# Alternating long and short query blocks, with GpSimd adding the two attention maps and TensorE transposing one tensor of the long blocks

## The chip, the cores and the metric

The kernel runs on one core of a Trainium2 chip. The metric is device time in microseconds (us) for one execution of the program; the kernel before took 1212.99 us, the median of three runs (1210.94 to 1213.68). The engines are called TensorE (PE in the profile, its weight loads PEld), VectorE (DVE), ScalarE (ACT), GpSimd (POOL) and SyncE (SP). All data are 32-bit floats, apart from masks and a few constants. The profiles show TensorE's granted clock as a share of full speed.

## The reference, cut to what matters

Eight sequences of 512 tokens with 128 features each go through one layer. First a causal attention with 16 heads of 8 features, which takes the difference of two softmaxes over the same queries:

```python
s1 = einsum('bhqd,bhkd->bhqk', q, k1) * SCALE      # causal mask on both
s2 = einsum('bhqd,bhkd->bhqk', q, k2) * SCALE
attn = softmax(s1) - sigmoid(lambda_logit) * softmax(s2)
attn = attn / max(sum(|attn|), 1e-6)
out = (attn @ v) @ Wo.T
x = layernorm(x + out)
```

Then a mixture of experts: eight experts of 128 -> 512 -> 128 with a SiLU, of which each token uses the two that its router scores highest, a residual and a second layer norm. Of the two softmaxes the kernel keeps the unnormalised exponentials e1 and e2 and works with e1 - c2*e2, where c2 is a ratio per row; dividing by the sum of absolute values makes the common factor drop out.

## The kernel before, in words

**Units, slots, rounds.** A sequence b is cut into 16 units j of 32 queries; because the attention is causal, unit j needs the first L = 32(j+1) keys. The 16 heads stand as four groups g of four heads, and four heads by 32 queries fill the 128 partitions. A unit with L up to 256 is *early* (short): it has two slots, each with two groups and both score sets. A unit with L over 256 is late (long): it has four slots, each with two groups and one score set. So a sequence has 8*2 + 8*4 = 48 slots, and each is worked in one *round* (`round_of`). Four units make a block of 128 queries; there are 32 blocks.

**What a round does.** The schedule is written by hand: the order of calls in `round_of` is the order on every engine's queue. One round (1) multiplies a finished unit by v (`times_v`, L490), (2) lets TensorE compute the scores of the next slot (`scores`, L327 and L336, into one of two PSUM buffers `sc`), (3) lets ScalarE copy the last piece's transposed attention out of PSUM (`evacuate`, L473, from the single buffer `pt`), (4) takes the negated row maxima of this slot on VectorE (`maxima`, L349 and L357), (5) transposes the piece that was combined in the round before (`transposes`, L448), (6) runs the VectorE steps that were put aside, (7) combines pieces (`combine`), (8) takes the exponentials on ScalarE with their row sums (`exps`, L367), and (9) issues one step of each side job: block tasks, routing, indirect DMAs on GpSimd, expert matmuls.

**A piece** is two groups of an early unit or one group of a late one. `combine` lets VectorE read e1 and e2 once to get the row sums of max(c2*e2, e1) (`junk`, L393), and then GpSimd scales e2 in place by -c2 (L403). The sum e1 - c2*e2 is not formed there: for every 128 keys `transposes` turns both tensors, the second accumulating on the first in PSUM, so that the sum comes out of TensorE already transposed. Keys that do not fill 128 are gathered by a GpSimd copy (`rest`, L417).

**After four units** (in the order of j, so every 16 or 8 rounds a block ends) the block's results stand in one PSUM bank `po`; ScalarE copies them (`oraw`, L508) and the block tasks (`block_tasks`: normalise, project with Wo, layer norm, router logits) follow, one per round, from the queue `misc`.

**Experts.** Blocks are collected in order into chunks of 6, 9, 9, 6 and 2 blocks. When a chunk is complete, `route_tasks` finds the two experts of each token, and for the first four chunks GpSimd sends every token's row to two places in a DRAM tensor `xs` with indirect DMAs (`send`, L777; two for each block, one per round, all sends of a chunk write the same tensor), so that the rows of one expert stand together. Three empty steps later `go` puts the chunk's expert tiles in the queue `experts`: 19 tiles of 128 rows for 6 blocks and 25 for 9. Each tile loads its weights and rows on SP's queue, is transposed (L871), multiplied (`pz`, L900), passed through the SiLU (L845, L847) and multiplied again (`pa`, L880). A pace, worked out from the expected arrival of the next chunk, says how many expert steps a round gets. Afterwards GpSimd fetches each token's two rows (`fetch`, L925). The last chunk of 2 blocks is dense: all its tokens go through all experts (`pzd`, `py`).

**Side jobs tied to a unit.** The next sequence's x is loaded when unit 6 opens, and its five projection tasks go into `misc` when unit 8 opens.

**Buffers.** The exponentials `et` (three of full width), `aT` (two), the sums of a block (three).

Of the kernel before, what the change touches and what calls it, by code (L numbers as in the profile page):

```python
# [20 lines left out]
def kernel(  # L21
# [22 lines left out]
    Q = 32  # L44
# [67 lines left out]
    with ExitStack() as actx:  # L112
# [3 lines left out]
        ep = actx.enter_context(tc.tile_pool(name="ep", bufs=3))  # L116
        tp = actx.enter_context(tc.tile_pool(name="tp", bufs=2))
        op = actx.enter_context(tc.tile_pool(name="op", bufs=1))
# [17 lines left out]
        stage = ep.tile([P, 2, NP, 128], F32, tag="et", name="stage")  # L136
# [69 lines left out]
        class Chunk:  # L206


            def __init__(self, n0, nb, sparse):
                self.n0, self.nb, self.sparse = n0, nb, sparse  # L210
                self.xh = self.lg = None
                if sparse:
                    self.nt = tiles_of(nb)
                    self.xs = dram.tile([self.nt * P, D], F32, name=f"xs_{n0}")
                    self.ys = dram.tile([self.nt * P, D], F32, name=f"ys_{n0}")
# [11 lines left out]
        zero = aw.tile([P, D], F32, name="zero")  # L227
        chunks, n0 = [], 0
        for nb in (6, 9, 9, 6):
            chunks.append(Chunk(n0, nb, True))  # L230
            n0 += nb
        for n0 in range(n0, NB, 2):
            chunks.append(Chunk(n0, 2, False))
        chunk_of = {n: c for c in chunks for n in range(c.n0, c.n0 + c.nb)}
# [59 lines left out]
        class Unit:  # L294


            def __init__(self, b, j, blk):
# [11 lines left out]
                self.et = ep.tile([P, NG, 2, T], F32, tag="et", name=f"et_{b}_{j}")  # L309
                self.aT = self.c2 = self.rest = None  # L310

# [73 lines left out]
            def combine(self, piece):  # L385
# [16 lines left out]
                for g in piece:  # L402
# [7 lines left out]
                    )  # L410
                for gs, lo, kw in self.blocks(piece):
                    if len(gs) > 1:
                        if self.rest is None:
# [4 lines left out]
                            self.rest[:, :, gs[0] * kw : (gs[-1] + 1) * kw].rearrange(  # L418
                                "p s (g l) -> p s g l", l=kw
                            ),  # L420
                            self.et[:, gs[0] : gs[-1] + 1, :, lo : lo + kw].rearrange(
# [17 lines left out]
            def transposes(self, piece):  # L439

                pt = ps_t.tile([P, 4, P], F32, tag="pt", name=f"pt_{self.b}_{self.j}_{piece[0]}")
                for x_, (gs, lo, kw) in enumerate(self.blocks(piece)):
                    for k in range(2):
                        if len(gs) == 1:
                            lhsT = self.et[:, gs[0], k, lo : lo + kw]
                        else:
# [6 lines left out]
                            start=(k == 0),  # L453
# [4 lines left out]
            def evacuate(self, piece, pt):  # L458
                if self.aT is None:
                    self.aT = tp.tile([P, NG * NT, P], F32, tag="aT", name=f"aT_{self.b}_{self.j}")  # L460
# [19 lines left out]
            def times_v(self):  # L480
# [3 lines left out]
                if "po" not in self.blk:  # L484
                    self.blk["po"] = ps_o.tile([P, JT, P], F32, tag="po", name=f"po_{self.b}_{self.i}")
                for kb in range(self.n):
                    kw = min(P, self.L - P * kb)
                    v, rows = (vr[kw], P) if kw in vr else (vt, kw)
                    for g in range(NG):
                        nc.tensor.matmul(  # L490
                            self.blk["po"][32 * g : 32 * g + 32, self.jj, :],
# [4 lines left out]
                        )  # L496

        def block_tasks(b, i, blk):
# [5 lines left out]
            lg, ci = ch.lg, n - ch.n0  # L504

            def reciprocals():
                s["oraw"] = op.tile([P, JT, P], F32, tag="oraw", name=f"oraw_{n}")
                nc.scalar.copy(s["oraw"], blk["po"])  # L508
# [14 lines left out]
            def normalise():  # L523
                pm = ps_m.tile([P, JT, P], F32, tag="pm", name=f"pmr_{n}")
                for jj in range(JT):
# [7 lines left out]
                        s["oraw"].rearrange("p j (h q) -> p j h q", q=Q),  # L533
# [280 lines left out]
        def last_tasks(ch, c, acc):  # L814

            n = ch.n0 + c
# [138 lines left out]
        def dense_tasks(ch):  # L955
# [6 lines left out]
            def hidden(e, half):  # L962
# [25 lines left out]
                silu_doubled(pz, h, name, *((tp, "aT") if e in whole else (hp, "th")))  # L988
# [57 lines left out]
        to_combine, to_transpose, to_evacuate, to_multiply = deque(), deque(), deque(), deque()  # L1046

        def after_blocks(u):
            u.times_v()
            if u.jj == JT - 1:  # L1050
                tasks = block_tasks(u.b, u.i, u.blk)

                tasks[0]()
                misc.extend(tasks[1:])
                n = u.b * NT + u.i
                ch = chunk_of[n]
                if n == ch.n0 + ch.nb - 1:
# [5 lines left out]

        def times():

            at, now, ends = [], 0.0, {}
            for n in range(NB):
                for j in range(n % NT * JT, (n % NT + 1) * JT):
                    L = (j + 1) * Q
                    now += 2 * time_of(4 * L) if L <= T // 2 else 4 * time_of(2 * L)  # L1070
                ends[n] = now
            seq = now / B
            for ch in chunks:

                behind = seq * (24 + (2 * ch.nb + 3 if ch.sparse else 0)) / 48
# [205 lines left out]
```

## Time and profile before

| what | us |
|---|---|
| median of three runs | 1212.99 |
| the profiled execution, device time | 1212.04 |
| its span | 1210.1 |
| TensorE busy | 1093.9 |
| VectorE busy | 927.1 |
| ScalarE busy | 780.4 |
| GpSimd busy | 526.8 |
| start of the span to the first exponentials | 19 |
| the eight sequences' attention, with side jobs | 1070 |
| after the last exponentials | 121 |

The profile lists the busy time of each engine, and it can be asked for the same in any stretch of the span; the last three rows come from the start of the first and the end of the last exponentials (L367). Matmuls are pipelined, and a busy TensorE is not TensorE at its peak: eight transposes of 296 ns each stand in 1.09 us. A group of instructions is listed by its line, with its number, its busy time, the mean of one, and the idle time of its engine ahead of it. The profiled execution was 1.94 us longer than its span and 0.95 us shorter than the median.

### The profile page before, as it was taken

The page shows a single profiled execution, that of the slowest core. Times are in us where ns is not written, and L with a number is a line of the kernel's source. Part 1 is how long each engine was busy: PE and PEld are TensorE (multiplying, and loading weights), DVE is VectorE, ACT ScalarE, POOL GpSimd, SP SyncE. Part 2 cuts the span into 40 slices and gives each one's busy share as a digit, 9 for nine tenths or more (in the row PEclk, how much of TensorE's full clock was granted, in tenths as well). Part 3 has the DMA queues.
Part 4 walks back from the last instruction along what each step waited for, and adds up shares of the span by engine and source line. Part 5 has one row for each costly group of instructions (what it writes and reads, how often), then busy time and mean ns, then how long its engine had stood idle before and what let it go on. Part 6 is the DMA issues. An engine that isn't in the chain of part 4 may idle for free.

```text
span 1210.1 us, 28192 instructions
## 1 busy us (share of the span) xinstructions
PE 1093.9 (90%) x9450; PEld 776.2 (64%) x9450; DVE 927.1 (77%) x2837; ACT 780.4 (64%) x2775; POOL 526.8 (44%) x935
## 2 busy tenths in 40 slices
PE   5999899989999899989998999988999989997686
PEld 3566565555666566666666666666667667777675
DVE  4688778777887887987887878887767898874556
ACT  3678767576777777766766867774567566662221
POOL 4343433463423442267464432333554652444333
PEclk7699969797999999989998999997899799998998
DMA  4400000110221112100322222221213344444762
GB/s 133 122 8 1 10 2 8 31 56 30 50 63 46 54 32 67 45 27 27 93 69 58 73 54 68 64 73 31 81 52 91 95 120 124 122 123 129 207 177 67
DMA packets 128895, 84.28 MB, mean 70 GB/s; under 512 B 22896, under 2 KB 114288, under 8 KB 128752
## 3 DMA queue, kind: packets, MB, share of 16 engines
q1 hardware_dynamic: 111952, 68.26, 20.2%
q0 software_dynamic: 3840, 7.87, 2.3%
q10 hardware_dynamic: 12960, 6.36, 1.8%
q8 instruction: 75, 1.23, 0.4%
q14 instruction: 68, 0.56, 0.2%
HBM read 63.31 MB, written 17.56 MB: 67 GB/s over the span
## 4 chain that ended last, share of the span: by engine, by line
PE 60%; DVE 16%; ACT 11%; issue 6%; POOL 4%; DMA 3%; ACTq 1%; POOLq 0%; SPq 0%; DVEq 0%
PE pt L448 19%; PE sc L327 13%; ACT et L367 7%; PE po L490 5%; PE pz L900 5%; PE pa L880 5%; PE sc_None L327 5%; DVE junk L393 2%; DVE nm L357 2%; PE pmo L541 2%; ACT aT L473 2%; DVE nm L349 2%; POOL et L403 1%; DVE hT L847 1%; POOL xs L777 1%
## 5 line engine op out<-in xcount | busy, mean ns | idle before, releaser
L403 POOL TENSOR_SCALAR et<-et,c 128x224 f32<-128x224 f32 (+15 forms) x512 | 270.9, 534 | 458.1 <-DVE junk L393 295.0
L448 PE MATMUL pt<-ident,et 128*128 128x128 f32 (+1 forms) x2048 | 326.7, 296 | 26.8 <-ACT aT L473 14.9
L448 PEld LDWEIGHTS pt<-ident,et 128*128 128x128 f32 (+1 forms) x2048 | 230.5, 145 | 159.6 <-issue 58.2
L367 ACT ACTIVATE et<-sc,nm 128x512 f32<-128x512 f32 (+7 forms) x512 | 300.4, 595 | 48.7 <-DVE nm L357 27.6
L357 DVE TENSOR_REDUCE nm<-sc 128x2 f32<-128x576 f32 (+7 forms) x256 | 252.0, 984 | 45.1 <-PE sc L336 44.6
L473 ACT COPY aT<-pt 128x384 f32<-128x384 f32 (+5 forms) x488 | 186.1, 407 | 134.5 <-PE pt L448 130.7
L393 DVE SCALAR_TENSOR_TENSOR junk<-et,c 128x224 f32<-128x224 f32 (+15 forms) x512 | 258.6, 505 | 9.6
L327 PE MATMUL sc<-kT,qb 32*128 32x384 f32 (+7 forms) x1024 | 246.8, 559 | 10.9 <-ACT et L367 9.6
L367 ACT ACTIVATE et<-sc_None,nm 128x256 f32<-128x256 f32 (+7 forms) x512 | 188.6, 387 | 32.0 <-DVE nm L349 22.0
L327 PE MATMUL sc_None<-kT,qb 32*128 32x512 f32 (+7 forms) x512 | 116.5, 535 | 21.8 <-ACT et L367 21.0
L900 PE MATMUL pz<-xgT,w 128*128 128x128 f32 x704 | 102.1, 291 | 18.8 <-DVE xgT L874 18.5
L349 DVE TENSOR_REDUCE nm<-sc_None 128x4 f32<-128x256 f32 (+7 forms) x128 | 96.1, 751 | 29.6 <-PE sc_None L336 29.3
L327 PEld LDWEIGHTS sc<-kT,qb 32*128 32x128 f32 x1024 | 78.3, 187 | 61.3 <-ACT et L367 27.4
L367 ACT ACTIVATION_READ_ACCUMULATOR et<-sc_None,nm 128x1 f32 x512 | 108.1, 211 | 0.0
L900 PEld LDWEIGHTS pz<-xgT,w 128*128 128x128 f32 x704 | 92.5, 204 | 23.6 <-DVE xgT L874 21.2
L367 ACT ACTIVATION_READ_ACCUMULATOR et<-sc,nm 128x1 f32 x512 | 103.9, 203 | 0.0
L880 PE MATMUL pa<-w,hT 128*128 128x128 f32 x704 | 98.1, 285 | 0.6 <-ACT ysb L890 0.6
L845 ACT ACTIVATE th<-pz 128x512 f32<-128x512 f32 x88 | 52.7, 599 | 68.9 <-PE pz L900 47.9
L880 PEld LDWEIGHTS pa<-w,hT 128*128 128x128 f32 x704 | 90.9, 202 | 1.3 <-ACT ysb L890 0.7
L777 POOL DMA_INDIRECT xs<-xh,row x60 | 65.9, 1099 | 46.9 <-DMA xs<-xh,row 31.3
L490 PE MATMUL po<-aT,vt 128*32 128x128 f32 (+1 forms) x2048 | 85.3, 290 | 0.0
L847 DVE SCALAR_TENSOR_TENSOR hT<-th,pz 128x512 f32<-128x512 f32 x88 | 60.2, 684 | 30.8 <-ACT th L845 30.6
(150 smaller groups left out, 1281.0 us busy)
## 6 DMA issues: line engine op xcount, KB each, us to landing
w<-in_w_dram SPq DMA_DIRECT2D x192, 256.0 KB
xg<-xs SPq DMA_DIRECT2D x88, 64.0 KB
ys<-ysb ACTq DMA_DIRECT2D x88, 64.0 KB
xs<-zero SPq DMA_DIRECT2D x2, 1600.0 KB
xs<-zero SPq DMA_DIRECT2D x2, 1216.0 KB
xt<-in_x_dram SPq DMA_DIRECT2D x8, 256.0 KB
out_dram<-ot SPq DMA_DIRECT2D x32, 64.0 KB
vr<-vt SPq DMA_DIRECT2D x32, 32.0 KB
```

The lines of the kernel that those rows point to most:

```text
L327: nc.tensor.matmul(parts[gi][:, :, :L], lhsT=qb[r, j].rearrange("p h q -> p (h q)"), rhs=kT[r, sets, :L], start=True, stop=False,)
L349: nc.vector.tensor_reduce(self.nm[:, g, :], sc.rearrange("p g (s l) -> p g s l", s=2)[:, :, :, : self.L], AX.X, ALU.max, negate=True,)
L357: nc.vector.tensor_reduce(self.nm[:, g, s], sc[:, :, : self.L], AX.X, ALU.max, negate=True)
L367: nc.scalar.activation(self.et[:, g, si, : self.L], sc[:, gi, lo : lo + self.L], AF.Exp, bias=self.nm[:, g, si : si + 1], accum_out=self.b ...
L393: nc.vector.scalar_tensor_tensor(junk[:, :L], self.et[:, g, 1, :L], self.c2[:, g : g + 1], self.et[:, g, 0, :L], ALU.mult, ALU.max, accum_ ...
L403: nc.gpsimd.tensor_scalar(self.et[:, g, 1, :L], self.et[:, g, 1, :L], self.c2[:, g : g + 1], -1.0, ALU.mult, ALU.mult,)
L448: nc.tensor.matmul(pt[: len(gs) * kw, x_, :], lhsT=lhsT, rhs=ident, is_transpose=True, start=(k == 0), stop=(k == 1),)
L473: nc.scalar.copy(self.aT[: rows[done], self.used + done : self.used + end, :], pt[: rows[done], done:end, :],)
L490: nc.tensor.matmul(self.blk["po"][32 * g : 32 * g + 32, self.jj, :], lhsT=v[:rows, kb, 32 * g : 32 * g + 32], rhs=self.aT[:rows, self.at[g ...
L777: nc.gpsimd.indirect_dma_start(ch.xs[:, :], bass.IndirectOffsetOnAxis(ap=ch.row[:, k, c : c + 1], axis=0), ch.xh[:, c, :], None,)
L880: nc.tensor.matmul(pm[:, 1, :], lhsT=hT[y][:, f, :], rhs=w[y][1][:, f, :], start=(f == 0), stop=(f == NF - 1),)
L900: nc.tensor.matmul(pz[:, f, :], lhsT=w[t][0][:, f * P : (f + 1) * P], rhs=xgT[t], start=True, stop=True,)
```

## The change

It changes the order of the rounds, the work of a late piece, and what follows from both.

- **Order.** `rounds_of` yields two rounds of a late unit and one of an early one in turn: units 15 and 0 together, then 14 and 1, down to 8 and 7. The two lengths of a pair add up to 544 keys. A sequence still has 48 rounds.
- **A late piece.** After scaling e2 by -c2, GpSimd adds e1 to it in place (`tensor_add`, 256 instructions on 288 to 512 columns). `transposes` and the `rest` copy then take the one tensor. Early pieces are as before. One piece is combined in each round.
- **Results of a unit.** `po` holds one unit; `keep` copies each with ScalarE (128x128, 128 times) into the block's `oraw`, in the round after `times_v`, in place of one 128x512 copy for each block.
- **Blocks** end in the order 3, 0, 2, 1 of each sequence: blocks 3 and 0 in its middle, 2 and 1 at its end. The chunks take blocks in that order.
- **Side jobs.** x of the next sequence is loaded when unit 3 opens (round 20 of 48, before: 12), and the projections are queued when unit 4 opens (round 26, before: 16). The estimate of a chunk's arrival is adapted (30 rounds behind in place of 24).
- **Buffers.** `et`: two of full width and two of half; `aT`: one of each width; `oraw` three; the sums four.

```diff
-        ep = actx.enter_context(tc.tile_pool(name="ep", bufs=3))
+        ep = actx.enter_context(tc.tile_pool(name="ep", bufs=2))
+        ap = actx.enter_context(tc.tile_pool(name="ap", bufs=1))
+        orp = actx.enter_context(tc.tile_pool(name="orp", bufs=3))
...
+        done = [b * NT + i for b in range(B) for k in range(NT // 2) for i in (NT - 1 - k, k)]
         for nb in (6, 9, 9, 6):
-            chunks.append(Chunk(n0, nb, True))
+            chunks.append(Chunk(done[n0 : n0 + nb], True))
...
+                self.added = not self.early
+                self.turned = slice(1 if self.added else 0, 2)
...
                         ALU.mult,
                         ALU.mult,
                     )
+                    if self.added:
+                        nc.gpsimd.tensor_add(
+                            self.et[:, g, 1, :L], self.et[:, g, 1, :L], self.et[:, g, 0, :L]
+                        )
...
-                    for k in range(2):
+                    for k in range(self.turned.start, 2):
...
+            def keep(self, po):
+                if "oraw" not in self.blk:
+                    self.blk["oraw"] = orp.tile([P, JT, P], F32, tag="oraw", name=f"oraw_{self.b}_{self.i}")
+                nc.scalar.copy(self.blk["oraw"][:, self.jj, :], po)
...
         def after_blocks(u):
-            u.times_v()
-            if u.jj == JT - 1:
+            to_keep.append((u, u.times_v()))
+
+        def keep(u, po):
+            u.keep(po)
+            u.blk["units"] += 1
+            if u.blk["units"] == JT:
+                misc.extend(block_tasks(u.b, u.i, u.blk))
...
+        def rounds_of():
+            for k in range(NJ // 2):
+                for n, late in enumerate((True, True, False, True, True, False)):
+                    yield (NJ - 1 - k, n - n // 3) if late else (k, n // 3)
...
-            left = now["left"] if now else 2
-            for _ in range(-(-len(to_combine) // left)):
+            for _ in range(min(len(to_combine), 1 if now else 2)):
...
-                for j in range(NJ):
-                    if b + 1 < B and j == 6:
+                for j, k in rounds_of():
+                    i = j // JT
+                    if j not in units:
+                        if b + 1 < B and j == 3:
                             load_x(b + 1)
-                    if b + 1 < B and j == 8:
+                        if b + 1 < B and j == 4:
                             misc.extend(projection_tasks(b + 1))
```

## The prediction

> **What bounds the kernel now.** I read the page's busy times first, then the busy time of each engine in ten stretches: the start, the eight sequences (cut at their first exponentials), and what follows the last exponentials. The columns are the stretch, its length, then busy time of PE, PEld, DVE, ACT, POOL, the granted clock, the DMA share and GB/s.
>
> ```profile
> PE 1093.9 (90%) x9450; PEld 776.2 (64%) x9450; DVE 927.1 (77%) x2837; ACT 780.4 (64%) x2775; POOL 526.8 (44%) x935
> ```
>
> ```profile
> 19.00:54.00 35.00, 32.07 (x157) 17.62 (x158) 21.78 (x87) 24.36 (x124) 12.13 (x31) 0.50 0.64 177
> 54.00:130.00 76.00, 73.75 (x690) 47.23 (x691) 64.65 (x176) 59.81 (x193) 29.57 (x51) 1.00 0.02 4
> 130.00:260.00 130.00, 119.50 (x973) 75.38 (x971) 101.05 (x320) 86.93 (x324) 60.71 (x100) 0.86 0.05 15
> 260.00:387.00 127.00, 120.92 (x1073) 81.76 (x1071) 100.43 (x297) 92.31 (x335) 46.75 (x88) 0.93 0.19 51
> 387.00:512.00 125.00, 117.64 (x1123) 82.84 (x1125) 103.60 (x318) 94.51 (x344) 46.06 (x87) 1.00 0.18 51
> 512.00:647.00 135.00, 123.37 (x1095) 84.97 (x1095) 112.93 (x348) 93.52 (x339) 82.00 (x124) 0.95 0.20 56
> 647.00:781.00 134.00, 125.91 (x1162) 90.83 (x1162) 105.05 (x312) 95.78 (x345) 47.39 (x89) 0.97 0.23 64
> 781.00:929.00 148.00, 135.27 (x1169) 97.22 (x1170) 111.24 (x342) 96.03 (x349) 67.57 (x107) 0.91 0.21 59
> 929.00:1089.00 160.00, 150.09 (x1359) 114.78 (x1358) 132.41 (x418) 105.91 (x372) 81.47 (x124) 0.96 0.41 118
> 1089.00:1210.00 121.00, 86.90 (x634) 78.77 (x634) 67.42 (x202) 28.67 (x56) 43.93 (x53) 0.91 0.52 145
> ```
>
> TensorE bounds the 1070 us of attention: 94% of the fourth sequence (117.64 of 125). VectorE is close behind with 103.60. The clock matters: the first 16 short rounds run at 0.50 although TensorE is busy 92% of them, and the 32 long rounds after them at 1.00. Behind the last exponentials, at 1089, lie 121 us of experts.
>
> The groups split by shape carry the prices, and GpSimd's and TensorE's rows in order of time show the last sends and the first tile of the last sparse chunk:
>
> ```profile
> L448 PE MATMUL pt<-ident,et 128*128 128x128 f32 x1792 | 294.4, 297 | 25.7 <-ACT aT L473 14.9 <-POOL et L403 8.9 <-issue 0.7
> L403 POOL TENSOR_SCALAR et<-et,c 128x512 f32<-128x512 f32 x32 | 30.9, 979 | 19.2 <-DVE junk L393 19.1
> L403 POOL TENSOR_SCALAR et<-et,c 128x480 f32<-128x480 f32 x32 | 21.3, 668 | 55.3 <-DVE junk L393 28.8 <-ACT et L367 12.3 <-PE pt L448 8.4
> L403 POOL TENSOR_SCALAR et<-et,c 128x288 f32<-128x288 f32 x32 | 16.2, 508 | 39.4 <-DVE junk L393 24.7 <-ACT et L367 12.3 <-ACT th L845 1.3
> L393 DVE SCALAR_TENSOR_TENSOR junk<-et,c 128x512 f32<-128x512 f32 x32 | 26.6, 832 | 0.8
> L393 DVE SCALAR_TENSOR_TENSOR junk<-et,c 128x480 f32<-128x480 f32 x32 | 22.8, 712 | 0.3
> ```
>
> ```profile
> 1071.80 1.24 POOL L777 DMA_INDIRECT xs<-xh,row  x1 [0.85 <-DMA xs<-xh,row]
> ...
> 1074.60 1.06 POOL L777 DMA_INDIRECT xs<-xh,row  x1 [0.41 <-DMA xs<-xh,row]
> ```
>
> ```profile
> 1086.65 1.09 PE L448 MATMUL pt<-ident,et 128*128 128x128 f32 x8
> ...
> 1094.00 1.97 PE L448 MATMUL pt<-ident,et 128*128 128x128 f32 x8 [0.68 <-ACT aT L473]
> 1095.76 1.91 PE L900 MATMUL pz<-xgT,w 128*128 128x128 f32 x8
> ```
>
> The reader sees three things: a send waits for the one before it (2.8 us apart), eight transposes take 1.09 us at full and 1.97 us at half clock, and the chunk's first tile starts 7 us behind the last exponentials, because its sends were over by then.
>
> **Part 1, transposes.** The late units have 102 blocks of keys per sequence, the early ones 38; one of two transposes goes for the 102. So 816 of 2,240 go (the built program has 1,424 left). At 1.09/8 = 0.136 us that is 111 us of TensorE time, 13.9 per sequence. TensorE's 117.6 in the fourth sequence becomes 103.7, level with VectorE's 103.6, which the change leaves alone. So 13.9 is a ceiling, and how much of it arrives depends on how well two level engines overlap.
>
> **Part 2, the added sums on GpSimd.** No row shows a two-input sum of this size. Bounds: one input on 288 to 480 columns takes 0.51 to 0.67 us, at 400 about 0.60; reading twice as much would be 1.20. I take the middle, 0.90: 256 x 0.90 = 230 us (154 to 307), 29 per sequence, all in GpSimd's idle time: 46 of 125 become 75, in the fifth sequence, with 18 sends, 82 become 111 of 135. The sum is queued between the scaling and the next piece; behind it wait the piece's transposes, the indirect DMAs and the power steps of the layer norms. In the long rounds the transposes start 0.9 to 1.4 us after the scaling, so a piece of 512 columns is just in time, and one behind a 1.1 us indirect DMA is not. The Trainium skill (GPSIMD Engine Reference, 3.1 Elementwise) gives 4497 ns for 2048 elements; by it my estimate is 0.88 at 400 columns, and the sum the same.
>
> **Part 3, collisions.** At 512 columns both VectorE's reading and GpSimd's scaling are dearer than the 480 row lets one expect: 832 against 712 and 979 against 668 ns. These are the pieces that come two to a round, where one group's reading overlaps the other's scaling. After the change pieces come one to a round, which removes this for the long ones (32 x 0.12 + 32 x 0.3 = 13 us, off TensorE's path); but GpSimd is at work most of the time, and a late sum meets the next reading. Bounds: none, or half of the 256 long readings delayed by 0.31 us, 40 us. I put 2 us per sequence in the overlap below. The Trainium skill (SBUF, Who interferes with whom) says that a VectorE instruction with two SBUF inputs and a GpSimd one that reads SBUF shut each other out; by it the long readings (2 per three rounds) and GpSimd's work would have to follow each other: 258.6/8 = 32 us of readings and 75 on GpSimd, 107 us per sequence, under the 118 I come to, so the sum would stay.
>
> **Part 4, the clock at the start.** Now the first 16 rounds are short and cheap, and cost 35 us at half clock; the 32 long ones run at full clock. Mixed from the start, rounds of scores and half as many transposes look to TensorE like the slow stretch. I expect half clock until the projections of round 26 bring dense matmuls: 28 rounds x 3.1 us (a long round at half clock: four score matmuls and masks 2.4, four transposes 1.0; a short one about 2.5) = 87, then 20 x 2.2 = 44: 131 against 111, +20. Below it stands 0, if the clock rises at once. The Trainium skill (TensorE: Matmul & The Clock Gate, What's actually happening) has full speed after one busy window of about 3.4 us; by it the 20 us are 0 and the total 20 lower. The row of 19 to 54, busy and yet at 0.50, speaks against it.
>
> **Part 5, the other seven sequences.** The second and third have few experts and a clock of 0.86 and 0.93 already; less TensorE work gives VectorE's bound or a lower clock: 0 and -2 (bounds -18 and +10). The fourth to seventh: about 60% of 13.9 arrives, -7, -8, -8, -9. The last is dense with experts: -4. Sum of the attention: +20 + 0 - 2 - 7 - 8 - 8 - 9 - 4 = -18.
>
> **Part 6, the end.** The last sparse chunk now ends with blocks 3 and 0 of the last sequence, 24 rounds before its end; before, 32. A unit's result also comes about eight rounds behind its last slot. In the built order all 12 sends stand behind the last long piece on GpSimd, whereas now they end 14 us before the last exponentials. From the last exponentials: seven pieces are left on GpSimd (4 x 1.2 + 1 = 6 to 7 us), 11 x 2.6 to the last send, 2.6 until it lands, 2 for the rows, 1 to the first `pz`: 41, rounded, against 7 now: +34. The 19 tiles then go without attention pieces between them, -3. +31 (bounds 20 and 45); nothing covers it, as the earlier chunk is paced to end with the attention.
>
> **Part 7, small moves.** 128 copies of 128x128 (0.27, the `ysb` row) for 32 of 0.59: +16 us on ScalarE, in its 36% idle time. The load of x (one DMA per sequence on SP, now among expert loads) comes six rounds before its use, the projections (with 8 DMAs on SP, 4 GpSimd steps) still over ten rounds before the next sequence; one `aT` buffer is free two rounds before its next use. Nothing each; if their cover goes, it shows as a wait of the projections for x, a few us per sequence.
>
> **Sum.** 1212.0 - 18 + 31 = 1225 us for the profiled execution; the median of the runs is 1 us above it.
>
> **The rivals.** (A) *The engines overlap and the clock holds*: the other side. Every sequence runs at 94% of its busiest engine: -5, -18, -13, -15, -15, -15, -19, -15 = -115; with +31: 1128 at best, 1170 in its middle. It decides from 31 us of attention gained on. For it: waits of TensorE are small today and VectorE has 17% free; against it: three engines in lock step within 10%, and the clock. (B) *GpSimd becomes the bound*: in the rounds with indirect DMAs (120) a long piece and a DMA make 0.6 + 0.9 + 1.1 = 2.6 us against 2.3 to 2.5 per round; with the 40 us of part 3: about 1265. (C) *It cancels*: gain and end within 2 us of each other, 1213. That the transposes stay is excluded by the built program.
>
> **How the numbers follow.** A measurement tells 0.2% (2.4 us) from no change. Forecast, slower by the end and the start: 0.37; B, 0.16; A, 0.41; C, 0.06. So faster 0.41, same 0.06, slower 0.53. The range goes from A's better half to B: 1140 to 1268; the forecast's own is 1212 to 1245.
>
> **What would show it.** Right: 1,424 transposes; the last exponentials near 1071 and 152 us behind them; all last sends behind them, 2.6 apart; a clock of 0.50 in the first 80 us; sums near 0.9 us. Wrong: last exponentials before 1058 (A), or a first sequence at full clock.

## The result, and the profile after

The changed kernel takes 1327.97 us (median of 4 runs, 1325.52 to 1337.15); the kernel before, on the same chip, 1213.34 (1210.94 to 1214.96). The ratio is 1.096, 95% interval 1.090 to 1.102: 115 us slower, where 1225 was forecast with a range of 1140 to 1268. The profiled execution took 1326.78 us with a span of 1325.1. Some executions of a kernel are over 1.5% longer than its fastest, at a lower clock: ratios here leave those out, while medians take in all runs. The experiments ran on several chips, each beside the kernel before, so kernels of different experiments are best compared by their ratios.

The page's busy times of the changed kernel (share of the span, instructions):

```profile
PE 1142.5 (86%) x8634; PEld 765.5 (58%) x8634; DVE 979.1 (74%) x2837; ACT 785.6 (59%) x2871; POOL 797.4 (60%) x1191
```

TensorE has 816 instructions fewer and is busy 49 us longer. GpSimd has 271 us more. The stretches of the changed kernel, cut as before at the first exponentials of each sequence and at the last ones (stretch, length, busy PE, PEld, DVE, ACT, POOL, granted clock, DMA share, GB/s); the first line is the beginning of the second:

```profile
20.00:81.00 61.00, 56.32 (x304) 28.78 (x306) 38.69 (x94) 39.84 (x153) 30.38 (x43) 0.50 0.36 101
20.00:155.00 135.00, 127.30 (x751) 70.72 (x753) 89.89 (x239) 84.59 (x325) 70.75 (x105) 0.58 0.18 48
155.00:292.00 137.00, 128.77 (x873) 76.57 (x871) 101.69 (x306) 88.21 (x337) 80.89 (x120) 0.68 0.02 5
292.00:432.00 140.00, 125.12 (x919) 76.60 (x917) 108.03 (x308) 90.99 (x342) 94.76 (x132) 0.77 0.16 45
432.00:563.00 131.00, 116.79 (x1004) 76.62 (x1004) 105.99 (x302) 94.49 (x356) 80.66 (x120) 0.92 0.16 45
563.00:717.00 154.00, 135.55 (x1013) 89.56 (x1009) 112.57 (x334) 94.88 (x354) 101.45 (x140) 0.79 0.15 42
717.00:861.00 144.00, 130.16 (x1055) 90.38 (x1053) 118.98 (x344) 96.65 (x358) 97.34 (x136) 0.85 0.24 67
861.00:1013.00 152.00, 135.97 (x1106) 93.79 (x1102) 120.77 (x345) 98.88 (x365) 99.33 (x140) 0.87 0.21 60
1013.00:1167.00 154.00, 139.50 (x1277) 105.84 (x1274) 137.32 (x408) 104.78 (x378) 102.44 (x142) 0.96 0.40 113
1167.00:1325.00 158.00, 93.84 (x630) 80.93 (x628) 76.02 (x234) 29.53 (x64) 60.58 (x75) 0.83 0.46 131
```

The attention grew from 1070 to 1147 us and the part behind the last exponentials from 121 to 158. The first sequence (135) and the end came about as forecast; sequences two to eight took 1012 where 921 was forecast and 959 was the time before. In all of these but the last the clock is lower than before, and TensorE is busy 90% of the time instead of 93%: in the fourth sequence 116.79 of 131 us at a clock of 0.92, before 117.64 of 125 at 1.00, although a third of its transposes went.

The groups of the changed kernel on GpSimd and then on VectorE, split by shape (busy us, mean ns of one, then idle time before it):

```profile
L424 POOL TENSOR_TENSOR et<-et 128x512 f32<-128x512 f32 x32 | 41.3, 1292 | 2.7
...
L424 POOL TENSOR_TENSOR et<-et 128x416 f32<-128x416 f32 x32 | 36.8, 1149 | 2.7
...
L424 POOL TENSOR_TENSOR et<-et 128x384 f32<-128x384 f32 x32 | 31.9, 996 | 2.7
...
L424 POOL TENSOR_TENSOR et<-et 128x288 f32<-128x288 f32 x32 | 25.4, 794 | 2.7
```

```profile
L405 DVE SCALAR_TENSOR_TENSOR junk<-et,c 128x512 f32<-128x512 f32 x32 | 31.1, 971 | 0.3
L405 DVE SCALAR_TENSOR_TENSOR junk<-et,c 128x480 f32<-128x480 f32 x32 | 26.5, 829 | 0.3
```

The sum takes 1.05 us in the mean (269 us in 256), and VectorE's readings became dearer (971 and 829 ns against 832 and 712). The waits of the changed kernel (engine, tile and line that waited, for what: us in all, times, longest):

```profile
POOL et L415 <- DVE junk L405: 239.0, 184, 14.4
...
PEld pt L464 <- POOL et L424: 112.2, 129, 3.0
...
PE pt L464 <- POOL et L424: 54.3, 70, 2.6
...
PEld pmr L546 <- POOL rexp L541: 22.9, 19, 12.2
...
PE pmr L546 <- POOL rexp L541: 18.2, 17, 11.9
```

The same in the kernel before, where the transposes wait for a scaling:

```profile
POOL et L403 <- DVE junk L393: 295.0, 198, 4.7
...
PEld pt L448 <- POOL et L403: 16.0, 28, 1.8
...
PE pt L448 <- POOL et L403: 9.7, 17, 1.6
```

A wait of the weight loads (PEld) and one of the matmuls (PE) for the same thing fall together in time, so they are not added: the transposes' two waits for the sum cover 112 us together, and in 54 of them no matmul ran. So TensorE now waits for GpSimd, most often for the sum, while GpSimd itself waits for VectorE's readings 239 us (before: 295): it is idle 40% of the time and late all the same. Such a place in the fourth sequence, from the rows of the changed kernel in order of time (start, duration, what it waited for in brackets):

```profile
500.30 0.64 DVE L405 SCALAR_TENSOR_TENSOR junk<-et,c 128x416 f32<-128x416 f32 x1
...
500.38 1.48 POOL L424 TENSOR_TENSOR et<-et 128x416 f32<-128x416 f32 x1
...
501.84 0.61 POOL L415 TENSOR_SCALAR et<-et,c 128x416 f32<-128x416 f32 x1
501.91 0.31 PEld L464 LDWEIGHTS pt<-ident,et 128*128 128x128 f32 x3 [1.11 <-POOL et L424]
501.91 0.55 PE L464 MATMUL pt<-ident,et 128*128 128x128 f32 x3 [0.75 <-POOL et L424]
...
502.53 1.07 POOL L424 TENSOR_TENSOR et<-et 128x416 f32<-128x416 f32 x1
```

A reading of VectorE began first, so the sum took 1.48 us instead of 1.07. The next piece's reading was over at 500.94, but its scaling starts at 501.84, behind the sum. TensorE waits 1.11 us for the sum.

The end, from the rows of GpSimd and TensorE in order of time:

```profile
1176.05 1.13 POOL L797 DMA_INDIRECT xs<-xh,row  x1 [0.18 <-issue]
...
1202.25 0.96 POOL L797 DMA_INDIRECT xs<-xh,row  x1 [1.54 <-DMA xs<-xh,row]
1204.74 0.96 POOL L797 DMA_INDIRECT xs<-xh,row  x1 [1.54 <-DMA xs<-xh,row]
```

```profile
1212.54 1.93 PE L920 MATMUL pz<-xgT,w 128*128 128x128 f32 x8
```

All twelve sends lie behind the last exponentials (1167), 2.6 us apart, and the first tile of the last sparse chunk comes 45 us behind the last exponentials.

### The profile page after: what moved, and what is told of

Same layout as the page of the kernel before. It is cut to its first block, busy times and chain, and to the rows that moved or that the text cites. A ratio compares the mean times of both kernels' runs of the same rounds, so it can differ in the third digit from the quotient of the medians.

```text
span 1325.1 us, 27029 instructions
## 1 busy us (share of the span) xinstructions
PE 1142.5 (86%) x8634; PEld 765.5 (58%) x8634; DVE 979.1 (74%) x2837; ACT 785.6 (59%) x2871; POOL 797.4 (60%) x1191
## 4 chain that ended last, share of the span: by engine, by line
PE 52%; DVE 22%; POOL 12%; issue 6%; ACT 5%; DMA 3%; SPq 0%; ACTq 0%; POOLq 0%; DVEq 0%
PE sc L339 12%; PE pt L464 12%; PE po L506 6%; DVE junk L405 5%; PE sc_None L339 5%; DVE nm L369 5%; POOL et L424 4%; PE pa L900 4%; PE pz L920 4%; ACT et L379 3%; POOL et L415 3%; PE pmo L561 2%; DVE hT L867 2%; POOL xs L797 1%; DMA xs<-xh,row 1%
## 5 line engine op out<-in xcount | busy, mean ns | idle before, releaser
L415 POOL TENSOR_SCALAR et<-et,c 128x416 f32<-128x416 f32 (+15 forms) x512 | 266.1, 524 | 349.3 <-DVE junk L405 239.0
L379 ACT ACTIVATE et<-sc,nm 128x288 f32<-128x288 f32 (+7 forms) x512 | 300.4, 594 | 88.6 <-DVE nm L369 72.4
L464 PE MATMUL pt<-ident,et 128*128 128x128 f32 (+1 forms) x1280 | 266.1, 335 | 62.5 <-POOL et L424 54.3
L339 PE MATMUL sc<-kT,qb 32*128 32x416 f32 (+7 forms) x1024 | 301.2, 672 | 18.5 <-ACT et L379 18.1
L369 DVE TENSOR_REDUCE nm<-sc 128x2 f32<-128x1024 f32 (+7 forms) x256 | 250.9, 981 | 86.7 <-PE sc L348 86.3
L405 DVE SCALAR_TENSOR_TENSOR junk<-et,c 128x416 f32<-128x416 f32 (+15 forms) x512 | 281.9, 550 | 9.2
L464 PEld LDWEIGHTS pt<-ident,et 128*128 128x128 f32 (+1 forms) x1280 | 160.6, 161 | 213.5 <-POOL et L424 112.2
L424 POOL TENSOR_TENSOR et<-et 128x512 f32<-128x512 f32 (+7 forms) x256 | 269.4, 1053 | 21.3
L339 PEld LDWEIGHTS sc<-kT,qb 32*128 32x128 f32 x1024 | 94.3, 225 | 75.0 <-ACT et L379 35.9
L945 POOL DMA_INDIRECT got<-ys,row x60 | 62.8, 1047 | 51.0 <-DVE x L955 32.4
```

Of the source, the lines that this page charges most:

```text
L339: nc.tensor.matmul(parts[gi][:, :, :L], lhsT=qb[r, j].rearrange("p h q -> p (h q)"), rhs=kT[r, sets, :L], start=True, stop=False,)
L369: nc.vector.tensor_reduce(self.nm[:, g, s], sc[:, :, : self.L], AX.X, ALU.max, negate=True)
L379: nc.scalar.activation(self.et[:, g, si, : self.L], sc[:, gi, lo : lo + self.L], AF.Exp, bias=self.nm[:, g, si : si + 1], accum_out=self.b ...
L405: nc.vector.scalar_tensor_tensor(junk[:, :L], self.et[:, g, 1, :L], self.c2[:, g : g + 1], self.et[:, g, 0, :L], ALU.mult, ALU.max, accum_ ...
L415: nc.gpsimd.tensor_scalar(self.et[:, g, 1, :L], self.et[:, g, 1, :L], self.c2[:, g : g + 1], -1.0, ALU.mult, ALU.mult,)
L424: nc.gpsimd.tensor_add(self.et[:, g, 1, :L], self.et[:, g, 1, :L], self.et[:, g, 0, :L])
```

## The experiments

Four explanations stood against each other. **C**: TensorE's clock fell because less work was left, and with it the gain went. **O**: the alternating order itself costs. **W**, called G in the first four expectations: the transposes wait for a sum that comes late. **P**: what costs is GpSimd's added work itself, whoever reads its result; later split into **X** (two-input work on GpSimd holds up VectorE's two-input work) and **Q** (in GpSimd's queue, everything behind the sums comes late).

### The order alone

```diff
-                self.added = not self.early
+                self.added = False
```

> The alternating order is kept, but the long units take both tensors through TensorE as before: no sum on GpSimd, 2,240 transposes. Theory C (the clock follows how densely TensorE is busy, and the removed transposes were what kept it up): clock in the attention back to 0.90 to 0.95, attention about 1070 to 1090 us, total 1225 to 1245. Theory G (the sum makes the transposes wait): the waits of transposes on GpSimd (166 us in the changed kernel) are gone, attention about 1080, total about 1230 to 1240. Theory O (the order itself costs): attention stays near 1140, total near 1310 to 1330.

Measured 1237.85 us, with runs from 1203.7 to 1248.6, beside 1219.65 for the kernel before: no ratio with an interval, about +1.5%. Profiled (1240.95 us): attention 1065 (first sequence 139, the other seven 927), then 154. So in this run the order costs nothing in the attention: it loses 28 us in the first sequence, regains 32 in the others (959 before), and costs 33 us at the end. O falls, except for the end; C and W named nearly the same numbers here and are not told apart.

### Without the sums

```diff
-                    if self.added:
+                    if False:
                         nc.gpsimd.tensor_add(
```

> The changed kernel without the 256 sums, one tensor still turned: the long units' attention lacks the first of its two parts, so the output is another. 1,424 transposes and no GpSimd work of 269 us. Theory C: TensorE has as little to do as in the changed kernel, so its clock stays at 0.75 to 0.85 and the total at 1280 to 1330. Theory G: the transposes no longer wait, attention at or below 1050, clock 0.9 or more, total 1150 to 1210. Theory O: 1290 to 1330, with a clock above 0.9.

Measured 1230.54 us, ratio 1.0099 (1.0049 to 1.0149). Profiled: attention 1052 (116 and 935), then 155; clock 0.854 in the span. Its busy times, beside those of the order alone:

```profile
PE 1076.8 (88%) x8634; PEld 724.9 (59%) x8634; DVE 927.6 (76%) x2837; ACT 777.8 (63%) x2871; POOL 517.4 (42%) x935
```

```profile
PE 1109.1 (89%) x9450; PEld 783.9 (63%) x9450; DVE 932.4 (75%) x2837; ACT 783.0 (63%) x2871; POOL 523.4 (42%) x935
```

Two things follow. Taking 816 transposes from TensorE, with a sum that costs nothing, is worth 7 us of 111 by the medians, and with the order alone at 1203.7 to 1248.6 and this kernel at 1220.3 to 1243.9 not even its sign is settled. In part that is because the clock falls from 0.905 to 0.854: TensorE is busy only 32 us less. And its matmuls of the scores wait 42 us for the exponentials, 32 with the order alone. Second, the sums cost 97 us (1328 against 1231; ratios 1.096 and 1.010), most of the loss. C's number (1280 to 1330) was too high and G's (1150 to 1210) too low: taking the sums away removes the loss, but no gain appears.

### The sums and both turns, and a matmul of no use

The first edit turns two tensors in the long units, so that TensorE has its 816 transposes back: the first one unsummed, then the sum over it (so not the same values, as the expectation has it, but the same work). The second puts one dense matmul ahead of each piece's transposes in the changed kernel.

```diff
-                    for k in range(self.turned.start, 2):
+                    for k in range(2):
...
-                            lhsT = self.rest[:, k, gs[0] * kw : (gs[-1] + 1) * kw]
+                            lhsT = self.rest[:, max(k, self.turned.start), gs[0] * kw : (gs[-1] + 1) * kw]
...
-                            start=(k == self.turned.start),
-                            stop=(k == 1),
+                            start=(k == 0 or self.added),
+                            stop=(k == 1 or self.added),
```

```diff
+                nc.tensor.matmul(
+                    pt.rearrange("p a b -> p (a b)"),
+                    lhsT=identb,
+                    rhs=identb.unsqueeze(1).to_broadcast([P, 4, P]),
+                    start=True,
+                    stop=True,
+                )
```

> The changed kernel with the sums, but each block of the long units is turned twice (the second overwrites the first with the same values): TensorE has its 816 transposes back, the wait on the sum is kept. Theory C: the clock comes back to about 0.9 and the total falls below the changed kernel's, 1260 to 1310. Theory G: the wait stays and 111 us of TensorE work come on top of it, partly hidden: 1330 to 1390. Theory O: 1320 to 1350.

> The changed kernel with one matmul of no use (bf16 identity by 512 columns, 0.21 us at full clock) ahead of the transposes of each piece, into the tile that they then overwrite: some 384 of them, 82 us of TensorE work that waits for nothing but its tile. Theory C: clock above 0.9 in the attention, total 1250 to 1300. Theory G: clock little changed, total 1330 to 1400. Theory O: 1330 to 1370.

Measured 1311.42 us (ratio 1.077, 1.068 to 1.086) and 1308.28 (1.0715, 1.064 to 1.079). More work for TensorE makes the changed kernel 17 and 20 us faster by the medians, 23 and 30 by the ratios; the clock in the attention goes from 0.80 to 0.91 and 0.89. Both lie above C's numbers and below G's: C holds for some 20 to 30 us of the 115, and the rest stays with a good clock. The first of the two can be set beside the order alone, which gives TensorE the same matmuls at the same clock in the attention (0.91 in both) and lacks only the sums: 1311 against 1238 us, and no run of the one is nearer than 59 us to one of the other. So C is not the main cause.

### Sums for which nobody waits

```diff
                         nc.gpsimd.tensor_add(
-                            self.et[:, g, 1, :L], self.et[:, g, 1, :L], self.et[:, g, 0, :L]
+                            self.et[:, g, 0, :L], self.et[:, g, 1, :L], self.et[:, g, 0, :L]
                         )
```

> The sums are made, at the same place in GpSimd's order and of the same size, but written into the other half of the unit's tile, which nothing reads afterwards; the transposes read the scaled half alone and wait for the scaling only (the long units' attention lacks its first part, as in the kernel without the sums, which took 1231 us). Theory W (the transposes wait for a late sum): the wait is gone, 1230 to 1250. Theory P (what costs is GpSimd's work itself: collisions with VectorE's readings, which grew from 505 to 550 ns, and the scaling queued behind the sum of the piece before): 1290 to 1330.

Measured 1313.18 us (1297.84 to 1330.58; ratio 1.072, 1.065 to 1.080). Only some 15 us below the changed kernel (29 by the ratios), and 83 above the kernel without sums (76): W falls as the main cause. Waits of TensorE's weight loads in this run, in which they read no sum:

```profile
PEld pt L464 <- POOL et L415: 50.0, 67, 2.3
...
PEld pmr L546 <- POOL rexp L541: 38.8, 23, 12.2
...
PEld pt L464 <- POOL rest L433: 27.3, 36, 2.1
...
PEld pt L464 <- POOL et L424: 17.7, 34, 1.0
```

and the same lines without the sums:

```profile
PEld pt L464 <- POOL et L415: 37.7, 65, 1.8
...
PEld pt L464 <- POOL rest L433: 18.1, 27, 1.7
...
PEld pmr L546 <- POOL rexp L541: 15.5, 11, 12.2
```

The wait for the sum itself (112 us in the changed kernel) is down to 18, which the profile still puts down to it. In its place TensorE waits for the next scaling, for the copies of remainders and for the spread reciprocals, which stand behind the sums in GpSimd's queue: its matmuls wait 22, 15 and 33 us for these, in the changed kernel 4, 4 and 18 beside the 54 for the sum.

### The transposes a round later

```diff
-            for _ in range(len(to_transpose)):
-                v, piece = to_transpose.popleft()
+            while to_transpose and (to_transpose[0][2] < rounds_done or not now):
+                v, piece, _ = to_transpose.popleft()
                 to_evacuate.append((v, piece, v.transposes(piece)))
+            rounds_done += 1
...
-                to_transpose.append((v, piece))
+                to_transpose.append((v, piece, rounds_done))
```

> The changed kernel, complete, with the transposes of each piece issued two rounds after its scaling instead of one. Theory W: one round (2.3 to 2.9 us) covers the sum, attention at 1050 to 1070 as in the kernel without sums, total 1205 to 1250. Theory P: little changes, 1300 to 1335.

Measured 1302.85 us (ratio 1.075, 1.068 to 1.083). The waits for the sum are nearly gone:

```profile
PEld pt L464 <- POOL et L424: 18.0, 30, 1.8
...
PE pt L464 <- POOL et L424: 4.9, 6, 1.2
```

That is 18 and 5 us instead of 112 and 54, and only 25 us come of it: P's 1300 to 1335, the second look that speaks against W. It speaks less clearly than the run before, because the later turn has a price of its own that no run separates: the exponentials now wait 94 and 48 us for the two kinds of maxima, 72 and 8 in the changed kernel.

### The sums in the old order

The kernel before with the same sum behind the scaling and one turned tensor in the long units.

```diff
+                self.added = not self.early
+                self.turned = slice(1 if self.added else 0, 2)
...
+                    if self.added:
+                        nc.gpsimd.tensor_add(
+                            self.et[:, g, 1, :L], self.et[:, g, 1, :L], self.et[:, g, 0, :L]
+                        )
...
-                    for k in range(2):
+                    for k in range(self.turned.start, 2):
```

> The kernel before, with its order (each sequence from its shortest block to its longest) and its buffers, and only the sums and the one turned tensor of the long units. The tail stays at 121 us. If order and sum add up (order +1 to +2%, all of it in the tail, sum +7%): 1280 to 1310. If the old order, where long pieces come one to a round in the last 32 rounds and two to a round at lengths of 288 to 512, makes GpSimd the bound there: above 1320. If the alternation was what made the sum dear: 1200 to 1250. Theories W and P both expect the first.

Measured 1337.99 us (1317.48 to 1347.72), beside 1212.92: in the median above the 1320 named for a GpSimd that binds more in the old order, but its two fastest runs, 1317 and 1330, lie on both sides of it. No ratio with an interval. In the profiled run (1329.76) the end is back at 121 us, and the attention takes 1188, against 1147 in the alternating order. So in these two profiles the alternation helps the sum, by some 41 us of attention, and gives 37 of them back at the end.

### Other work in the place of the sum

Two runs vary what GpSimd does for nobody: two scalings with one input for each sum, and a sum over half of the columns.

```diff
-                        nc.gpsimd.tensor_add(
-                            self.et[:, g, 1, :L], self.et[:, g, 1, :L], self.et[:, g, 0, :L]
-                        )
+                        for k in range(2):
+                            nc.gpsimd.tensor_scalar(
+                                self.et[:, g, 0, :L],
+                                self.et[:, g, 1, :L],
+                                self.c2[:, g : g + 1],
+                                -1.0,
+                                ALU.mult,
+                                ALU.mult,
+                            )
```

```diff
+                        h = L // 2
                         nc.gpsimd.tensor_add(
-                            self.et[:, g, 1, :L], self.et[:, g, 1, :L], self.et[:, g, 0, :L]
+                            self.et[:, g, 0, :h], self.et[:, g, 1, :h], self.et[:, g, 0, :h]
                         )
```

> As in the run where nobody waits for the sum, but each sum is replaced by two more scalings with one input, some 0.6 us each, 308 us in all against 269 (results that nothing reads; the long units' attention lacks its first part). In that run the VectorE instructions with two SBUF inputs that met a sum were stretched by some 48 us in all, while those that met a scaling were not. Theory X (the sum holds up VectorE): without two-input work on GpSimd the time falls back towards the kernel without sums, 1235 to 1260. Theory Q (GpSimd is late: its scalings, exponent rows and sends stand behind 269 us more): as late or later, 1310 to 1345.

> As in the run where nobody waits for the sum (1313), with sums over half of the columns, some 0.57 us each and 145 us in all (the long units' attention lacks its first part). If the cost is in proportion to GpSimd's added time: 1275. Theory Q, a queue that is late only when a round's work is more than the round: well below that, 1235 to 1255. Theory X: a short sum that starts on time ends before VectorE's next reading, so it meets few of them, 1235 to 1265; the stretch of VectorE's instructions tells the two apart: below 15 us by X, while by Q it doesn't matter.

Measured 1345.77 us (ratio 1.1085, 1.105 to 1.112) and 1255.48 (1.028, 1.022 to 1.035). The busy times with two scalings:

```profile
PE 1156.3 (86%) x8634; PEld 772.6 (58%) x8634; DVE 965.0 (72%) x2837; ACT 782.2 (58%) x2871; POOL 843.9 (63%) x1447
```

VectorE is busy 965 us, less than the 991 with the whole sums for which nobody waits, and yet the kernel is 33 us slower: GpSimd's 48 us more decide, not the kind of work. That is Q, at the upper end of its 1310 to 1345. X is not refuted as a share of it: VectorE's readings still meet the scalings at times (778 ns at 480 columns, against 719 without sums and 860 with them). Half a sum, added GpSimd time 160 us, costs 25 us where a whole one, 279 us, costs 83: convex, as a queue would have it. This run does not tell Q from X: 1255 is the upper end of Q's 1235 to 1255 and inside X's 1235 to 1265.

The chain that ended last, as shares of the span by engine: without sums, with sums for which nobody waits, and with two scalings:

```profile
PE 49%; DVE 28%; ACT 9%; issue 6%; POOL 4%; DMA 3%; SPq 0%; ACTq 0%; POOLq 0%; DVEq 0%
```

```profile
PE 51%; DVE 24%; POOL 10%; issue 6%; ACT 6%; DMA 2%; SPq 0%; ACTq 0%; POOLq 0%; DVEq 0%
```

```profile
PE 51%; DVE 20%; POOL 15%; issue 6%; ACT 4%; DMA 3%; SPq 0%; ACTq 0%; POOLq 0%; DVEq 0%
```

GpSimd's share of the chain goes from 4% to 10% and 15%: 49, 133 and 201 us.

### Half of the sums, and sums without the scaling

```diff
-                self.turned = slice(1 if self.added else 0, 2)
+                self.turned = slice(0, 2)
...
-                    if self.added:
+                    if self.added and g % 2 == 0:
+                        full = L // P * P
                         nc.gpsimd.tensor_add(
-                            self.et[:, g, 1, :L], self.et[:, g, 1, :L], self.et[:, g, 0, :L]
+                            self.et[:, g, 1, :full], self.et[:, g, 1, :full], self.et[:, g, 0, :full]
                         )
...
-                    for k in range(self.turned.start, 2):
+                    first = 1 if self.added and gs[0] % 2 == 0 and len(gs) == 1 else 0
+                    for k in range(first, 2):
```

```diff
                 for g in piece:
-                    nc.gpsimd.tensor_scalar(
+                    if self.early:
+                        nc.gpsimd.tensor_scalar(
```

> A complete kernel in the changed order in which only every other group of the long units is summed, over its whole blocks of 128 keys: 128 sums, some 120 us, and 352 transposes fewer; the other groups go through TensorE with both tensors. Halfway between the order alone (1238) and the changed kernel (1328) would be 1283. By theory Q the time goes by how much GpSimd has to do, convexly (busy 517 us: 1231; 678: 1255; 796: 1313; 844: 1346): at some 645 us it gives 1235 to 1258. The direct wait of the transposes for the sum, if that counts, adds up to 8 us. Below 1213 it would beat the kernel before, which none of the theories expects.

> The changed kernel with all its sums, which the transposes wait for, but without the scaling of the long units' second tensor (their attention is the sum of both parts unscaled): GpSimd does 154 us less, some 643 us. Theory Q, by GpSimd's total and whatever the kind of work: 1240 to 1262, though each round still has its sum of 1.05 us and its transposes wait for it. Theory W (the wait for the sum itself) and theory X (two-input work holds up VectorE): the sums are all there, so 1290 to 1325.

The first is not quite the complete kernel that its expectation calls it: at the lengths 352 and 480 the last 96 keys of every other group miss their first part. Measured 1246.56 us (ratio 1.022, 1.009 to 1.035) and 1249.27 (1.024, 1.012 to 1.036), both inside Q's numbers. The second keeps every sum, with two inputs and with transposes that wait for it, and is 79 us faster than the changed kernel, with 168 us less work on GpSimd (629 against 797): W and X had 1290 to 1325.

### One step taken off GpSimd

```diff
-                nc.gpsimd.tensor_copy(s["rexp"], rd.unsqueeze(3).to_broadcast([P, JT, NG, 32]))
+                nc.scalar.copy(s["rexp"], rd.unsqueeze(3).to_broadcast([P, JT, NG, 32]))
```

> The changed kernel, complete, with one thing moved: the 32 copies that spread a block's reciprocals (rexp, 1 us each on GpSimd) are made by ScalarE, which is idle for 40% of the span. Theory Q in its sharper form (what stands late in GpSimd's queue holds TensorE up through whatever waits for it): TensorE's 41 us of waits of pmr for rexp go, and GpSimd has 32 us less; 1285 to 1310. If those waits are covered by other work (TensorE would have waited for something else then): 1318 to 1332.

Measured 1311.63 us (ratio 1.076, 1.064 to 1.087), between the two numbers named: 16 us below the changed kernel by the medians, 25 by the ratios. The expectation's 41 us add the waits of the weight loads (23) and of the matmuls (18), which fall together, so the wait was worth 23 at most. The gain fits that, and it fits the 13 us that 24 us less on GpSimd are worth at the upper rate of the table below; this run does not tell the two apart.

All kernels in the changed order by GpSimd's busy time (VectorE's beside it, from the page of each profiled run; time is the median, and the ratio is to the kernel before on the same chip):

| kernel | GpSimd busy | VectorE busy | time | ratio |
|---|---|---|---|---|
| no sums, one turn | 517 | 928 | 1231 | 1.010 |
| order alone, two turns | 523 | 932 | 1238 | none |
| sums without scaling | 629 | 959 | 1249 | 1.024 |
| every other group | 649 | 954 | 1247 | 1.022 |
| half sums, nobody waits | 678 | 945 | 1255 | 1.028 |
| changed, one step off GpSimd | 773 | 983 | 1312 | 1.076 |
| whole sums, nobody waits | 796 | 991 | 1313 | 1.072 |
| changed, transposes a round later | 796 | 1011 | 1303 | 1.075 |
| changed | 797 | 979 | 1328 | 1.096 |
| two scalings, nobody waits | 844 | 965 | 1346 | 1.109 |

From 517 to 678 the time rises by about 0.15 us per microsecond of GpSimd work, from 678 to 844 by about 0.55. VectorE's column does not order the times: 965 stands beside 1346 and 1011 beside 1303. By its median none of these kernels beats the one before. Since even a sum that cost nothing left 1231, 1% above it, none of this kind can be expected to without a shorter end.

## Why the prediction was wrong

**Part 1**, 13.9 us per sequence as a ceiling: the 816 transposes went as worked out, but the ceiling was taken at full clock. With the sum free they brought 7 us in all (1238 to 1231), less than the runs scatter. **Part 5**, "about 60% of 13.9 arrives", is the first step that failed: sequences two to eight took 927 us with both turns and 935 with one. What the profiles show in place of the gain is a lower clock (0.905 to 0.854) and longer waits for the exponentials (32 to 42 us).

**Part 2** is the step that failed most. The price of one sum was a little low: 1.05 us against 0.90, 269 us against 230, inside its bounds. The estimate from the Trainium skill (GPSIMD Engine Reference, 3.1 Elementwise), 0.88 at 400 columns, is low too: 0.996 at 384 and 1.149 at 416. What failed is "all in GpSimd's idle time". GpSimd was 60% busy, and much of its idle time is time in which it waits for VectorE's next reading (239 of some 530 us); once that comes, scaling, sum, remainder, reciprocals and sends follow one another, and TensorE waits for each. The prediction named who is queued behind the sum and gave it no price. It was 83 us when nobody read the sums, and some 15 more for reading them (76 and 29 by the ratios). How much of the 83 is the queue itself, and how much the collisions with VectorE's readings and the lower clock that came with it, these runs show only in part.

**Part 3**: the scaling at 512 columns fell from 979 to 692 ns, as said. The reading did not fall: 832 became 971, and 712 at 480 columns became 829. All readings together grew from 258.6 to 281.9 us, 23 more: above the 16 (2 per sequence) taken, inside the bound of 40. The 258.6 us that the prediction calls the long readings are those of all pieces, short ones too. VectorE as a whole is busy 52 us longer, and how much of it lies on the path is not settled by these runs.

**Part 4**: right in its number, 131 against 135, but in part by luck. The forecast was half clock to about 107 us and full clock after that. The two stretches behind the 61 us at 0.50 shown above:

```profile
81.00:107.00 26.00, 23.58 (x176) 13.63 (x172) 20.86 (x54) 18.63 (x67) 17.52 (x25) 0.89 0.05 9
107.00:155.00 48.00, 47.40 (x277) 28.31 (x275) 30.34 (x92) 26.11 (x105) 22.85 (x38) 0.52 0.00 1
```

So the clock rose earlier, and fell back to 0.52 where full clock was expected. Nor is the +20 the order's alone: the order alone gave 139, without the sums it was 116, and other runs in this order lie between.

**Part 6**: right in mechanism and near in size: 45 us from the last exponentials to the first tile against 41, and +37 against +31, inside 20 to 45. The order alone gives 33 of it, and the old order with the sums has 121 again.

**Part 7**: right. 128 copies of the raw outputs for 32 cost ScalarE 35 us instead of 19. The projections wait for x once, 5.7 us, at the start of the program, as before (5.9): the later load costs nothing.

**The rivals.** B was the right one, GpSimd as the bound, at 1265: 63 us too little. It counted only the 120 rounds with an indirect DMA as full and added the collisions; but the first two sequences, which have no indirect DMA, take 272 us with the sums and 243 without, so other rounds pay too. A fell in both its halves: TensorE is busy 90% of sequences two to eight, not 94%, and the clock does not hold.

## What to carry to other kernels

An engine's idle time is no room for more work if it is the wait for the step ahead of it in every round: ask what stands behind the new instruction in that engine's queue, and who waits for each of those. Moving work from a fast engine to a slow one needs the round's time on the slow one, 0.6 + 1.05 us and all its other steps, and not its share of the span. Where weight loads and matmuls wait for the same thing, the profile shows one wait on two rows: don't add them. Taking work from TensorE can be worth little even where it is the bound, because the granted clock can fall with it (here 0.905 to 0.854): try it first with the replacement left out.

## What was not expected of the hardware

**TensorE's clock and less work.** At the same order and with the sums, 816 transposes more gave a clock of 0.91 in the attention instead of 0.80, and 17 us less (23 by the ratios); 384 matmuls of no use gave 0.89 and 20 us less (30). TensorE was busy 92% of the 61 us at 0.50 and 99% of the 48 us at 0.52 shown above. The Trainium skill (TensorE: Matmul & The Clock Gate, What's actually happening) lets one busy window of about 3.4 us release the clock; a matrix engine that is busy by the profile's rows did not meet that here.

**A sum and a reading shut each other out.** Told from the rows' overlaps in the run in which nobody waits for the sums: readings of 480 columns that met a sum took 1139 ns in the mean and the others 714, with 601 ns of overlap; VectorE's maxima, which read PSUM, took 1223 ns at 1024 columns with a sum beside them and 1222 without. Where the reading was first, the sum was stretched (1.48 for 1.07 us above): in that run sums of 416 columns took 1.45 us in the mean behind a reading (5 of 32), and 1.06 where the sum was first (5) or alone (22). The Trainium skill (SBUF — State Buffer, Who interferes with whom) says that a VectorE instruction with two SBUF inputs and a GpSimd instruction that reads SBUF contend, and that the one that was issued first goes on: the trace agrees for the sum, though the delay is less than the overlap (425 of 601 ns for the readings above). The one-input scaling bears the delay where it comes second: in that run scalings of 288 columns took 801 ns when they met a reading (7 of 32, most of them second) and 505 when not, while readings of 288 columns that met only a scaling took 508 ns and the others 512.

**The same program at several clocks.** The order alone ran from 1203.7 to 1248.6 us on one chip, with a clock of 0.932 in the fastest run and 0.897 in the slowest. Differences of 1% between kernels with such a clock need many runs.
